# Two layers of feed-forward and attention on one core: attention's first tiles and maxima are issued within the feed-forward's last steps, and ScalarE sends the rows of the maxima

## The chip, the core and the metric

The kernel runs on one core of a Trainium2 chip. The core has TensorE (PE: matrix products, whose weight loads PEld overlap), VectorE (DVE), ScalarE (ACT), GpSimd (POOL) and SyncE (SP, which here only issues DMA transfers). Each engine works through its own instructions in order; they meet through semaphores. The metric is the device time of one execution in microseconds, median of the runs.

## What is computed

The input `x` has 2048 positions of 256 features, in f32. It goes through two "macaron" layers:

```
x = x + 0.5 * ffn0(layernorm(x));  x = x + attn0(layernorm(x));  x = x + 0.5 * ffn0(layernorm(x))   # layer 0: f0, attention, f1
x = x + 0.5 * ffn1(layernorm(x));  x = x + attn1(layernorm(x));  x = x + 0.5 * ffn1(layernorm(x))   # layer 1: f2, attention, f3
```

- `ffn0`: weights rounded to three values per group of 64, gate and up products to 1024 features, silu(gate) * up, RMS norm, down product.
- `ffn1`: the same gate and up form in f32, of each four hidden values the two with the largest magnitude are kept, then the down product.
- `attn0`, `attn1`: causal attention with 16 heads of 16 features. Layer 0 adds an ALiBi bias (slope of the head times key position minus query position); layer 1 has biases on q, k, v and output, and rotates q and k by position. Softmax, product with v, output projection.

## The kernel before

**Tiling.** Features lie on the partitions, positions along the free axis. Positions are cut into four chunks of 512 (`NCH`, `CH`), a chunk into four tiles of 128 (`T`). Attention works on 16 groups: group n is chunk n // 4 of the queries and four of the heads (n % 4). The phases follow each other: feed-forward f0, attention of layer 0, feed-forwards f1 and f2 in one run, attention of layer 1, f3.

**Feed-forward.** `feed_forwards` (L435) walks through the chunks, and through eight steps `f` per chunk. A step issues the gate and up products of 128 hidden features (L306 in layer 0: six pairs, as x is split in three bf16 parts; L281 in layer 1, f32), ScalarE's silu (L317) and VectorE's product (L318). In layer 0, VectorE also takes the parts of h (L334, L329), ScalarE squares (L339) and GpSimd sums (L340). The chunk's down products (L361 or L292) come in the next chunk's steps as a "tail". In layer 1, `sparsify` (L385) does the choice of two in four, with comparisons on VectorE (L394) and sums on GpSimd. Layer norms of the next phase run beside this from a list `background`. After each step a hook is called: `beside0` in f0, `beside1` in f1 and f2.

**Attention's preparation.** `attention` is a generator. Its first `next` opens the pool `ka` and yields another generator, `first()` (L618), which does chunk 0's work: `prep_qk(0, "k")`, `prep_qk(0, "q")`, `prep_v(0)`. `prep_qk` (L521) projects (L536, two halves), splits the f32 result in three bf16 parts (ScalarE L544 or L578, VectorE L545 or L579, ScalarE L580, GpSimd L581), and SyncE writes these to scratch in DRAM in six transfers (L585). Layer 1 comes with a bias (L547), a swap of the two 64-partition halves by DMA (L556) and the rotation (VectorE L571 and L577, GpSimd L575) ahead of the split. The hooks advance `first()` by one yield per step: in f0 in chunk 3's steps, in f2 from chunk 2's fifth step on. `attend` (L1032) runs what is left of it when the feed-forward has ended.

**Attention.** Then pools `kv` and `ap` are opened in the feed-forward's memory. `load` (L636) reads a group's q tile and a k tile (96 rows: head features in six product terms) back from DRAM, and constant rows below them (L640, L645). Query maxima come first: `mx_unit` (L663) takes scores with queries on the partitions (`pq`, L671, and a mask product L679), and VectorE reduces each 128x512 tile (L682). When a group has all its maxima, `mx_end` (L684) makes three bf16 parts of their negatives, and `mx_turn` (L699) transposes them on TensorE (L704), ScalarE copies (L712), and SyncE sends three rows into the q tile (L714), so that the second score product subtracts the maximum by itself. That second product has keys on the partitions (`st_pair`, L725: `pst`, L733), ScalarE takes the exponential (`pT`, L753), and four small products per head group add to the output (`pav`, L768), which VectorE and GpSimd divide by the sum (L789, L793, L794).

**What sets the order.** On the four compute engines the program's order is the order of the code (`manual_schedule`); only SyncE's transfers are ordered by the tile framework. `slots` (L829) lists one slot for each group and key block of 128. `maxima` (L835) puts units of maxima on slots. Slot -1 held group 0's four tiles and three tiles of group 1, seven units in all, ahead of the first slot (L912); after each of these units one step of chunk 1's preparation was taken. In the slots, `step` advances the preparation of the next chunk, and `need` drains it as far as a load asks for.

**Buffers that matter.** PSUM has two pairs of banks (`ps2`: gate/up products and `pst`), three single banks (`ps3`: `pq`, projections, means, down products, transposed maxima) and one bank for sums (`ps1`). The `kd` and `q` rings have four tiles each in `kv`.

Of the kernel before, what the change touches and what calls it, by code (L numbers as in the profile page):

```python
# [26 lines left out]
G = 4  # L27
# [19 lines left out]
def macaron_kernel(ctx: ExitStack, tc: tile.TileContext, a, out):  # L47
# [37 lines left out]
        )  # L85


    ident = cpool.tile([P, P], F32, name="ident")
    make_identity(nc, ident)
    ident_b = cpool.tile([P, P], BF16, name="ident_b")  # L90
    nc.vector.tensor_copy(ident_b, ident)

    mask_qk = cpool.tile([P, P], BF16, name="mask_qk")
    mask_kq = cpool.tile([P, P], BF16, name="mask_kq")
# [395 lines left out]
    def attention(layer, following):  # L490
# [9 lines left out]
        with ExitStack() as st:  # L500
# [20 lines left out]
            def prep_qk(c, what):  # L521

                ready(c)
                if what == "k" and c > 0:
                    nc.gpsimd.memset(va[c], 1.0)
                at = 0 if what == "q" else DC
                name = f"{layer}_{what}{c}"
                dn = ka.tile([P, DC, CH], F32, tag="dn", bufs=2 - layer, name=f"dn{name}")
                pt = [
                    ka.tile([P, DC, CH], BF16, tag=f"part{j}", bufs=1, name=f"p{j}{name}")  # L530
                    for j in range(3)
                ]
                for i in range(DC):
                    pp = ps_one(f"pp{name}_{i}")
                    for dc in range(DC):
                        nc.tensor.matmul(  # L536
                            pp,
                            lhsT=wqkv[:, dc, (at + i) * P : (at + i + 1) * P],
                            rhs=xns[c][:, dc, :],
                            start=dc == 0,  # L540
                            stop=dc == DC - 1,
                        )
                    if layer == 0:
                        nc.scalar.copy(pt[0][:, i, :], pp)  # L544
                        nc.vector.tensor_tensor(dn[:, i, :], pp, pt[0][:, i, :], ALU.subtract)  # L545
                    else:
                        nc.scalar.activation(  # L547
                            dn[:, i, :], pp, AF.Identity, bias=b_qk[:, at + i : at + i + 1]
                        )
                    if i == 0:  # L550
                        yield
                if layer == 1:

                    sw = ka.tile([P, DC, CH], F32, tag="sw", bufs=1, name=f"sw_{what}{c}")
                    for o in range(2):
                        nc.sync.dma_start(  # L556
                            out=sw[o * 64 : o * 64 + 64, :, :],
                            in_=dn[64 - o * 64 : 128 - o * 64, :, :],
                        )
                    if turns.get("of") != c:  # L560
                        turns["of"] = c
                        turns["cs"] = ka.tile(
                            [P, 2, CH], F32, tag="cs", bufs=1, name=f"cs_{what}{c}"
                        )
                        nc.sync.dma_start(
                            out=turns["cs"], in_=a["cos_sin"][:, :, c * CH : (c + 1) * CH]
                        )
                    cs = turns["cs"]
                    yield
                    yield  # L570
                    nc.vector.tensor_tensor(  # L571
                        dn, dn, cs[:, 0:1, :].to_broadcast([P, DC, CH]), ALU.mult
                    )
                    for i in range(DC):
                        nc.gpsimd.tensor_tensor(sw[:, i, :], sw[:, i, :], cs[:, 1, :], ALU.mult)  # L575
                    yield
                    nc.vector.tensor_tensor(dn, dn, sw, ALU.add)  # L577
                    nc.scalar.copy(pt[0], dn)  # L578
                    nc.vector.tensor_tensor(dn, dn, pt[0], ALU.subtract)  # L579
                nc.scalar.copy(pt[1], dn)  # L580
                nc.gpsimd.tensor_tensor(pt[2], dn, pt[1], ALU.subtract)  # L581
                for j in range(3):
                    for m, part in enumerate(Q_PARTS if what == "q" else K_PARTS):
                        if part == j:
                            nc.sync.dma_start(  # L585
                                out=parts[what, c][:, m, :, :].rearrange("i p t -> p i t"),
                                in_=pt[j],
                            )
                done.add((what, c))
                yield  # L590
# [24 lines left out]
                        done.add(("v", c))  # L615
                    yield

            def first():  # L618
                nc.gpsimd.memset(va[0], 1.0)
                yield  # L620
                for work in (prep_qk(0, "k"), prep_qk(0, "q"), prep_v(0)):
                    yield from work

            yield first()
            kv = st.enter_context(tc.tile_pool(name=f"kv{layer}", bufs=1))
            ap = st.enter_context(tc.tile_pool(name=f"at{layer}", bufs=2))
            va += [values(kv, c) for c in range(1, NCH)]
            acc = ps_acc(f"pav{layer}")
            zts = {}
            zs = {}  # L630


            qs = {}
            ks = {}

            def load(n, kc):  # L636
                c, g = divmod(n, G)

                def stack(to, what, of, extra):
                    nc.sync.dma_start(  # L640
                        out=to[0:RM],
                        in_=parts[what, of][g // 2]
                        .rearrange("m (d u) t -> (m d) u t", u=HB)[:, g % 2 * 4 : g % 2 * 4 + 4, :],
                    )
                    nc.sync.dma_start(out=to[RM:rows], in_=extra[0 : rows - RM])  # L645

                need("k", kc)
                ks[n, kc] = kv.tile(
                    [P, 4, CH], BF16, tag="kd" if kc == c else "ko", bufs=4 if kc == c else 5,
                    name=f"k{layer}_{n}_{kc}",  # L650
                )
                stack(ks[n, kc], "k", kc, a["k_rows"][c - kc])
                if n not in qs:
                    need("q", c)
                    qs[n] = kv.tile([P, 4, CH], BF16, tag="q", bufs=4, name=f"q{layer}_{n}")
                    stack(qs[n], "q", c, a["q_rows"][g])


# [4 lines left out]
            def mx_unit(n, t, kc, heads):  # L663

                c, g = divmod(n, G)
                if n not in mxs:
                    mxs[n] = ap.tile([P, T, 4, NCH], F32, tag="mx", bufs=4, name=f"mx{layer}_{n}")
                w = (t + 1) * P if kc == c else CH
                for hh in heads:
                    pq = ps_one(f"pq{layer}_{n}_{t}_{kc}_{hh}")[:, 0:w]  # L670
# [13 lines left out]
            def mx_end(n):  # L684


                c = n // G
                ng = ap.tile([P, T, 3, 4], F32, tag="neg", name=f"neg{layer}_{n}")
                nc.vector.tensor_reduce(
                    ng[:, :, 0, :], mxs.pop(n)[:, :, :, 0 : c + 1], AX.X, ALU.max, negate=True  # L690
                )
                top = ng.bitcast(BF16).rearrange("p t m (h two) -> p t m h two", two=2)[..., 1]
                for m in range(2):
                    nc.vector.tensor_tensor(
                        ng[:, :, m + 1, :], ng[:, :, m, :], top[:, :, m, :], ALU.subtract
                    )
                negs[n] = top

            def mx_turn(n):  # L699
# [3 lines left out]
                for t in range(T):  # L703
# [4 lines left out]
                        start=True,  # L708
                        stop=True,
                    )  # L710
                qx = ap.tile([12, CH], BF16, tag="qx", bufs=2, name=f"qx{layer}_{n}")
                nc.scalar.copy(qx, pt)  # L712
                for m in range(3):
                    nc.sync.dma_start(out=qs[n][RM + m : RM + m + 1, :, :], in_=qx[4 * m : 4 * m + 4, :])  # L714
                turned_max.add(n)


            def banks(name, apart):
# [161 lines left out]
            def need(*what):  # L880
                while what not in done:
                    assert preps, what
                    step()

            left = {}
            for units in maxima.values():
                for u in units:
# [17 lines left out]

            def load_to(slot):
                while uses and uses[0][1] <= slot:
                    load(*uses.popleft()[0])

            load_to(-1)  # L910
            preps.extend((prep_qk(1, "k"), prep_qk(1, "q"), prep_v(1)))
            for unit in maxima[-1]:  # L912
                mx_next(unit, (0, 1, 2, 3))
                step()
                now[0] += 1
                run_due()

            unsummed = deque()
            pairs = [0]
# [92 lines left out]

    def begin(layer, following):
        att = attention(layer, following)
        begun[:] = att, next(att)

    def beside0(s, at, f):
        if not quants and not begun:
            raw_scope.close()
            begin(0, "f1")  # L1020
        if at == NCH - 1:
            next(begun[1], None)

    def beside1(s, at, f):
        if s == 1 and at == 0 and f == FC // 2:
            own.close()
            ffn0_scope.close()
            begin(1, "f3")
        if s == 1 and (at == NCH - 1 or at == NCH - 2 and f >= FC // 2):
            next(begun[1], None)  # L1030

    def attend():  # L1032
        att, first = begun
        for _ in first:
            pass
        next(att, None)
        begun.clear()

# [126 lines left out]
```

## Time and profile before

| what | value |
|---|---|
| median of 3 runs | 1954.04 us (1952.93 to 1957.03) |
| profiled execution | 1957.69 us; its span 1955.7 us |
| TensorE | 1761.4 us busy, 90% of the span, mean granted clock 0.96 |
| VectorE | 1361.6 us, 70% |
| ScalarE | 894.2 us, 46% |
| GpSimd | 458.4 us, 23% |
| DMA | 93.10 MB, mean 48 GB/s |
| reductions of the maxima (L682) | 1280, 708.6 us, mean 603 ns |
| exponentials (L753) | 614, 542.6 us, mean 896 ns |
| rows of the maxima sent (L714) | 96 transfers of 4.0 KB, issued by SyncE |

The profile is of one execution. Busy time is that of instructions at work; an engine's idle time is put down to what released it ("releaser"), such as another engine's line or a DMA. "Granted clock" is the share of full speed that TensorE was allowed. In a timeline a row is a run of like instructions: start, length, engine, line, operation, out<-in, shape, and in brackets the idle time before it with its releaser. SPq and ACTq rows are the times in which SyncE or ScalarE issued a DMA.

### The profile page before, as it was taken

How to read it: one execution, taken by the hardware profiler on the slowest of the kernel's cores; microseconds unless marked ns; L12 is line 12 of the kernel's file. 1: busy time of each engine (PE TensorE's matmuls, PEld its weight loads, DVE VectorE, ACT ScalarE, POOL GpSimd, SP SyncE). 2: the span in 40 equal slices, each digit the busy share in tenths (PEclk: the TensorE clock that was granted, in tenths of full speed). 3: DMA queues.
4: the chain of work that ended last, by engine and by line, in shares of the span. 5: the costliest groups of instructions: out<-in, count | busy, mean ns of one | idle time of the engine just before them, and what ended most of it. 6: DMA issues, size and time to landing. Idle time of an engine off the chain costs nothing. (4 is left out here: it accounts for less than half of the span.)

```text
span 1955.7 us, 26994 instructions
## 1 busy us (share of the span) xinstructions
PE 1761.4 (90%) x10684; PEld 726.5 (37%) x10684; DVE 1361.6 (70%) x2384; ACT 894.2 (46%) x1112; POOL 458.4 (23%) x418
## 2 busy tenths in 40 slices
PE   5699789999999999789999876898999999998997
PEld 1233344433433333333444333433333333333443
DVE  7866377787788883666575655868877888825664
ACT  4343254555555668334422312445555656673220
POOL 3455321101000000455453432211111000003422
PEclk9799899999999999989999986999999999999999
DMA  4000252213211000200000115222122110000000
GB/s 129 1 1 33 82 148 83 73 54 102 62 45 46 28 28 2 73 1 0 1 11 0 54 61 158 82 73 92 52 69 86 43 43 26 18 1 0 11 11 22
DMA packets 50510, 93.10 MB, mean 48 GB/s; under 512 B 5424, under 2 KB 33072, under 8 KB 50128
## 3 DMA queue, kind: packets, MB, share of 16 engines
q1 hardware_dynamic: 49296, 89.28, 14.8%
q10 hardware_dynamic: 1088, 2.10, 0.3%
q8 instruction: 84, 1.38, 0.3%
q14 instruction: 42, 0.34, 0.1%
HBM read 59.51 MB, written 27.26 MB: 44 GB/s over the span
## 5 line engine op out<-in xcount | busy, mean ns | idle before, releaser
L682 DVE TENSOR_REDUCE mx<-pq 128x1 f32<-128x512 f32 (+3 forms) x1280 | 708.6, 603 | 158.5 <-PE pq L679 91.2
L753 ACT ACTIVATE pT<-pst 128x1024 f32<-128x1024 f32 (+3 forms) x614 | 542.6, 896 | 334.9 <-PE pst L733 196.8
L671 PE MATMUL pq<-k,q 105*128 105x512 bf16 (+7 forms) x1280 | 378.8, 353 | 74.7 <-DVE mx L682 52.3
L733 PE MATMUL pst<-q,k 99*128 99x512 bf16 (+7 forms) x1280 | 357.7, 354 | 5.1 <-ACT pT L753 4.2
L768 PE MATMUL pav<-pT,va 128*32 128x256 f32 (+1 forms) x4608 | 352.4, 382 | 5.2 <-DVE yt L789 5.0
L281 PE MATMUL pg_f<-xn,wgu 128*128 128x512 f32 x512 | 229.8, 602 | 11.5 <-DVE hr_f L318 11.5
L794 POOL TENSOR_TENSOR zt<-yt,rd 128x64 f32<-128x64 f32 x128 | 38.4, 300 | 795.2 <-DVE rd L793 795.1
L733 PEld LDWEIGHTS <-k 105*128 105x128 bf16 (+1 forms) x1280 | 101.5, 98 | 254.1 <-issue 218.4
L317 ACT ACTIVATE sl_f<-pg_f 128x512 f32<-128x512 f32 x128 | 76.0, 594 | 251.8 <-PE pg_f L281 175.0
L671 PEld LDWEIGHTS <-q 105*128 105x128 bf16 (+1 forms) x1280 | 124.5, 100 | 148.0 <-issue 44.3
L306 PE MATMUL pg_f<-xn,wgu 128*128 128x512 bf16 x512 | 156.2, 413 | 19.5 <-DVE wgu L170 6.8
L768 PEld LDWEIGHTS pav<-pT,va 128*32 128x32 f32 x4608 | 93.8, 108 | 208.7 <-issue 174.8
L281 PEld LDWEIGHTS pg_f<-xn,wgu 128*128 128x128 f32 x512 | 98.6, 193 | 136.9 <-issue 121.0
L306 PEld LDWEIGHTS <-wgu 128*128 128x128 bf16 x768 | 77.7, 101 | 166.9 <-issue 74.7
L292 PE MATMUL po_f<-h_f,wd 128*128 128x512 f32 x256 | 116.3, 608 | 17.3 <-DVE h_f L418 17.3
L340 POOL TENSOR_TENSOR ss_f<-ss_f,sq_f 128x512 f32<-128x512 f32 x56 | 91.1, 1628 | 111.5 <-ACT sq_f L339 111.3
L679 PE MATMUL pq<-mask_qk,ident_b 128*128 128x128 bf16 x512 | 107.3, 227 | 0.0
L741 PE MATMUL pst<-mask_kq,ident_b 128*128 128x128 bf16 x512 | 103.1, 222 | 0.0
L306 PE MATMUL pg_f<-xm_f,wgu 128*128 128x512 bf16 x256 | 85.3, 416 | 14.0 <-DVE xm_f L238 14.0
L318 DVE TENSOR_TENSOR h_f<-sl_f,pg_f 128x512 f32<-128x512 f32 x64 | 43.6, 682 | 76.4 <-ACT sl_f L317 76.3
L789 DVE STREAM_TRANSPOSE yt<-pav 128x128 f32<-128x128 f32 x128 | 39.8, 311 | 76.7 <-PE pav L768 76.7
L394 DVE TENSOR_TENSOR ge_f<-h_f 128x1536 bf16<-128x1536 f32 (+2 forms) x48 | 67.6, 1437 | 28.0 <-ACT h_f L387 28.0
(132 smaller groups left out, 1802.5 us busy)
## 6 DMA issues: line engine op xcount, KB each, us to landing
k<-dk SPq DMA_DIRECT2D x80, 384.0 KB
dk<-p_k SPq DMA_DIRECT2D x48, 256.0 KB
dq<-p_q SPq DMA_DIRECT2D x48, 256.0 KB
q<-dq SPq DMA_DIRECT2D x32, 384.0 KB
x<-in_xT ACTq DMA_DIRECT2D x4, 512.0 KB
raw<-in_w_gu SPq DMA_DIRECT2D x8, 256.0 KB
wgu<-in_w_gu SPq DMA_DIRECT2D x1, 2048.0 KB
cs_k<-in_cos_sin SPq DMA_DIRECT2D x4, 512.0 KB
```

The source lines that it names most:

```text
L281: nc.tensor.matmul(pg[:, half, :], lhsT=wgu[:, dc, half * F + f * P : half * F + (f + 1) * P], rhs=xn[:, dc, :], start=dc == 0, stop=dc == ...
L292: nc.tensor.matmul(po, lhsT=w[:, f, dc * P : (dc + 1) * P], rhs=h[:, f, :], start=f == 0, stop=f == FC - 1,)
L306: nc.tensor.matmul(pg[:, half, :], lhsT=wgu0[:, dc, half * F + f * P : half * F + (f + 1) * P], rhs=xp[part][:, dc, :], start=part == 0 an ...
L317: nc.scalar.activation(sl, pg[:, 0, :], AF.Silu)
L340: nc.gpsimd.tensor_tensor(ss, ss, sq, ALU.add)
L671: nc.tensor.matmul(pq, lhsT=qs[n][0:rows, hh, t * P : (t + 1) * P], rhs=ks[n, kc][0:rows, hh, 0:w], start=True, stop=kc < c,)
L679: nc.tensor.matmul(pq[:, w - P : w], lhsT=ident_b, rhs=mask_qk, start=False, stop=True)
L682: nc.vector.tensor_reduce(mxs[n][:, t, hh, kc : kc + 1], pq, AX.X, ALU.max)
L733: nc.tensor.matmul(ps[i][:, lo:CH], lhsT=ks[n, kc][0:rows, hh, t * P : (t + 1) * P], rhs=qs[n][0:rows, hh, lo:CH], start=True, stop=kc < c,)
L741: nc.tensor.matmul(ps[i][:, lo : lo + P], lhsT=ident_b, rhs=mask_kq, start=False, stop=True)
L753: nc.scalar.activation(pT[:, :, lo:CH], pair[:, :, lo:CH], AF.Exp, scale=0.25)
L768: nc.tensor.matmul(acc[hh * SLOT : (hh + 1) * SLOT, a:b], lhsT=va[kc][:, t, v0 : v0 + SLOT], rhs=pTs[hh // 2][:, hh % 2, a:b], start=kb == ...
```

## The change

1. `first()` now has more in it: after chunk 0's k and q it issues the loads of groups 0 and 1 (`load(0, 0)`, `load(1, 0)`), after v the seven units of maxima that were in slot -1, in halves of two heads with a yield after each, `mx_end` and `mx_turn` of group 0, and then chunk 1's k and q preparation.
2. A new `go_on` takes two yields per step, from the fifth step of chunk 2 on, for both layers. `attend` runs `first()` only until the maxima are done; what is left of it goes to the head of `preps`.
3. So that the loads can come before `kv` exists, groups with n % 4 of 0 and 1 have their k and q tiles in `ka`, two of each; 2 and 3 have two of each in `kv`. The maxima, negatives and `qx` are in `ka` too, with 3, 1 and 1 buffers instead of 4, 2 and 2.
4. The three transfers of a group's maxima rows are issued by ScalarE instead of SyncE, for all groups.
5. The ones in `va` of chunks 1 to 3 are set at attention's start instead of in `prep_qk`, and the bf16 identity is made directly.

```diff
-    ident = cpool.tile([P, P], F32, name="ident")
-    make_identity(nc, ident)
     ident_b = cpool.tile([P, P], BF16, name="ident_b")
-    nc.vector.tensor_copy(ident_b, ident)
+    make_identity(nc, ident_b)
...
+            pools = [ka]
+            def ring(n, other=False):
+                return pools[0 if other or n % 4 > 1 else -1]
...
-                need("k", kc)
-                ks[n, kc] = kv.tile(
-                    [P, 4, CH], BF16, tag="kd" if kc == c else "ko", bufs=4 if kc == c else 5,
+                ks[n, kc] = ring(n, kc < c).tile(
+                    [P, 4, CH], BF16, tag="kd" if kc == c else "ko", bufs=2 if kc == c else 5,
...
-                    need("q", c)
-                    qs[n] = kv.tile([P, 4, CH], BF16, tag="q", bufs=4, name=f"q{layer}_{n}")
+                    qs[n] = ring(n).tile([P, 4, CH], BF16, tag="q", bufs=2, name=f"q{layer}_{n}")
...
-                    nc.sync.dma_start(out=qs[n][RM + m : RM + m + 1, :, :], in_=qx[4 * m : 4 * m + 4, :])
+                    nc.scalar.dma_start(out=qs[n][RM + m : RM + m + 1, :, :], in_=qx[4 * m : 4 * m + 4, :])
...
+            def first():
+                nc.gpsimd.memset(va[0], 1.0)
+                yield
+                for work in (prep_qk(0, "k"), prep_qk(0, "q")):
+                    yield from work
+                load(0, 0)
+                yield from prep_v(0)
+                load(1, 0)
+                for n, t in FIRST:
+                    for heads in ((0, 1), (2, 3)):
+                        mx_unit(n, t, 0, heads)
+                        yield
+                    if (n, t) == (0, T - 1):
+                        mx_end(0)
+                        yield
+                        mx_turn(0)
+                        yield
+                done.add("maxima")
+                for work in (prep_qk(1, "k"), prep_qk(1, "q")):
+                    yield from work
+            FIRST = [(0, t) for t in range(T)] + [(1, t) for t in (2, 1, 0)]
...
-            load_to(-1)
-            preps.extend((prep_qk(1, "k"), prep_qk(1, "q"), prep_v(1)))
-            for unit in maxima[-1]:
-                mx_next(unit, (0, 1, 2, 3))
-                step()
-                now[0] += 1
-                run_due()
+                    (n, kc), _ = uses.popleft()
+                    if (n, kc) not in ks:
+                        need("k", kc)
+                        need("q", n // G)
+                        load(n, kc)
+            preps.extend((beginning, prep_v(1)))
...
+    def go_on(s, at, f):
+        if at == NCH - 1 or at == NCH - 2 and f >= FC // 2:
+            for _ in range(2):
+                next(begun[1], None)
...
     def attend():
-        att, first = begun
-        for _ in first:
-            pass
+        att, first, done = begun
+        while "maxima" not in done:
+            next(first)
```

More of the change, by code (lines that the diff above doesn't have):

```diff
@@ L523, in prep_qk @@
                 ready(c)
-                if what == "k" and c > 0:
-                    nc.gpsimd.memset(va[c], 1.0)
                 at = 0 if what == "q" else DC
@@ L616, in prep_v @@
                     yield
[L618 to L630, printed above, removed]
+            pools = [ka]
             qs = {}
             ks = {}
+            def ring(n, other=False):
+                return pools[0 if other or n % 4 > 1 else -1]
             def load(n, kc):
@@ L666, in mx_unit @@
                 if n not in mxs:
-                    mxs[n] = ap.tile([P, T, 4, NCH], F32, tag="mx", bufs=4, name=f"mx{layer}_{n}")
+                    mxs[n] = ka.tile([P, T, 4, NCH], F32, tag="mx", bufs=3, name=f"mx{layer}_{n}")
                 w = (t + 1) * P if kc == c else CH
@@ L687, in mx_end @@
                 c = n // G
-                ng = ap.tile([P, T, 3, 4], F32, tag="neg", name=f"neg{layer}_{n}")
+                ng = ka.tile([P, T, 3, 4], F32, tag="neg", bufs=1, name=f"neg{layer}_{n}")
                 nc.vector.tensor_reduce(
@@ L710, in mx_turn @@
                     )
-                qx = ap.tile([12, CH], BF16, tag="qx", bufs=2, name=f"qx{layer}_{n}")
+                qx = ka.tile([12, CH], BF16, tag="qx", bufs=1, name=f"qx{layer}_{n}")
                 nc.scalar.copy(qx, pt)
                 for m in range(3):
-                    nc.sync.dma_start(out=qs[n][RM + m : RM + m + 1, :, :], in_=qx[4 * m : 4 * m + 4, :])
+                    nc.scalar.dma_start(out=qs[n][RM + m : RM + m + 1, :, :], in_=qx[4 * m : 4 * m + 4, :])
                 turned_max.add(n)
+            def first():
[19 more added lines that the diff above has]
+            FIRST = [(0, t) for t in range(T)] + [(1, t) for t in (2, 1, 0)]
+            beginning = first()
+            yield beginning, done
+            kv = st.enter_context(tc.tile_pool(name=f"kv{layer}", bufs=1))
+            ap = st.enter_context(tc.tile_pool(name=f"at{layer}", bufs=2))
+            pools.insert(0, kv)
+            va += [values(kv, c) for c in range(1, NCH)]
+            for c in range(1, NCH):
+                nc.gpsimd.memset(va[c], 1.0)
+            acc = ps_acc(f"pav{layer}")
+            zts = {}
+            zs = {}
             def banks(name, apart):
@@ L883, in need @@
                     step()
+            assert sorted(maxima.pop(-1)) == sorted((n, t, 0) for n, t in FIRST)
             left = {}
@@ L907, in load_to @@
                 while uses and uses[0][1] <= slot:
-                    load(*uses.popleft()[0])
-            load_to(-1)
-            preps.extend((prep_qk(1, "k"), prep_qk(1, "q"), prep_v(1)))
-            for unit in maxima[-1]:
-                mx_next(unit, (0, 1, 2, 3))
-                step()
-                now[0] += 1
-                run_due()
+                    (n, kc), _ = uses.popleft()
[4 more added lines that the diff above has]
+            preps.extend((beginning, prep_v(1)))
             unsummed = deque()
@@ L1014, in begin @@
         att = attention(layer, following)
-        begun[:] = att, next(att)
+        begun[:] = att, *next(att)
+    def go_on(s, at, f):
+        if at == NCH - 1 or at == NCH - 2 and f >= FC // 2:
+            for _ in range(2):
+                next(begun[1], None)
     def beside0(s, at, f):
@@ L1020, in beside0 @@
             begin(0, "f1")
-        if at == NCH - 1:
-            next(begun[1], None)
+        go_on(s, at, f)
     def beside1(s, at, f):
@@ L1028, in beside1 @@
             begin(1, "f3")
-        if s == 1 and (at == NCH - 1 or at == NCH - 2 and f >= FC // 2):
-            next(begun[1], None)
+        if s == 1:
+            go_on(s, at, f)
     def attend():
-        att, first = begun
-        for _ in first:
-            pass
+        att, first, done = begun
+        while "maxima" not in done:
+            next(first)
         next(att, None)
```

## The prediction

> **What bounds the kernel now.** I read the busy time by stretch first, then TensorE's waits in the two stretches that hand a feed-forward over to attention, then the timelines. Columns of the first fence: stretch, length, busy time of PE, PEld, DVE, ACT, POOL, granted TensorE clock, DMA share, GB/s.
>
> ```profile
> 150.00:267.00 117.00, 96.33 (x381) 43.92 (x380) 62.13 (x93) 35.03 (x55) 45.75 (x30) 0.91 0.26 81
> 267.00:812.00 545.00, 519.20 (x4266) 207.21 (x4265) 411.33 (x834) 317.12 (x388) 49.14 (x85) 0.99 0.19 60
> ...
> 1050.00:1224.00 174.00, 137.38 (x378) 63.57 (x377) 98.61 (x139) 41.86 (x48) 63.03 (x42) 0.86 0.26 77
> 1224.00:1778.00 554.00, 519.15 (x4190) 207.48 (x4189) 408.45 (x822) 312.80 (x375) 55.85 (x90) 0.98 0.17 52
> ```
>
> TensorE sets the time almost everywhere (95% and 94% busy in the two attentions). Only at the two hand-overs does it not: 20.7 us idle of 117 in layer 0 and 36.6 of 174 in layer 1, with the clock at 0.91 and 0.86. So the change is judged there. Waits in these stretches (total, times, longest), layer 0, then layer 1:
>
> ```profile
> PE pq L671 <- DMA q<-in_q_rows: 8.7, 1, 8.7
> PE pss_f L353 <- POOL ss_f L340: 4.0, 1, 4.0
> PE pg_f L306 <- DVE xm_f L238: 2.2, 1, 2.2
> ```
>
> ```profile
> PE pq L671 <- DVE mx L682: 12.6, 5, 8.1
> PE po_f L292 <- DVE h_f L418: 10.3, 1, 10.3
> PE pg_f L281 <- DVE hr_f L318: 5.9, 1, 5.9
> PE pq L671 <- DMA q<-in_q_rows: 4.4, 1, 4.4
> ```
>
> The change aims at the first line of layer 0: the first score tile waits 8.7 us for q and k, whose pool opens only when the feed-forward has ended. The price of a long gap stands right behind it:
>
> ```profile
> 240.25 0.27 PE L671 MATMUL pq<-k,q 105*128 105x128 bf16 x1 [8.71 <-DMA q<-in_q_rows]
> ...
> 241.27 3.78 PE L536 MATMUL pp_k<-xn,wqkv 128*128 128x512 f32 x4
> ...
> 247.11 1.98 PE L536 MATMUL pp_k<-xn,wqkv 128*128 128x512 f32 x4
> ```
>
> The same four rows (two f32 products) take 3.78 us after the gap and 1.98 when warm: 1.9 us more, and about 2 us in all before full speed returns. What a q tile needs between its projection and its first use, in SyncE's queue and in the chain of waits:
>
> ```profile
> 201.71 4.99 SPq L585 DMA_DIRECT2D dq<-p_q  x6
> ```
>
> ```profile
> 1230.05 5.23 DMA q<-dq
> ```
>
> The q projection ended at 200.9, the six writes of its parts to DRAM were issued up to 206.7, and a read back takes 5.2 us from issue to use (also 5.5 at 234.71). Nothing of this was on TensorE's path before: the feed-forward ran on for 24 us. That is the cover that the change takes away.
>
> **The moved steps, layer 0.** The instruction orders show it: TensorE works in order, and chunk 0's q now ends one and a half steps before the first score tile, which stands ahead of the next gate/up product. I count from the start of chunk 2's fifth gate/up product (151.1 before). A gate/up step is 2.7 us, a projection half or v half 1.72, a mean 0.9. Then q's second half ends at 15.9; v 1.7, gate/up 2.7 and v 1.7 follow, so TensorE reaches score tile (0,0) at 22.0. The q chain meanwhile: ScalarE has chunk 1's Square first and converts at 18.4 to 19.0; VectorE has chunk 3's split (1.2+1.3) first and subtracts till 20.6; ScalarE's cast (1.04) till 21.7; GpSimd's subtraction (2.14) till 24.3; last write issued 24.8, landed 27.3 (estimate: 2.5, as DMA traffic of the dq writes before died out about 2 us after the last issue), read 5.2: 32.5. **TensorE stalls 10.5 us in the midst of the feed-forward**, and 2.0 cold.
>
> Next, each moved step brings up to four score tiles, but ps3 has three banks. The fourth tile waits until VectorE has reduced the first, and VectorE's reductions are queued behind the step's silu, product, difference and last part (0.6+3x0.7) and often a transpose. Going through the order I get waits of 1.7, 3.1, 0.8, 2.7 and 3.2 us at chunk 3's steps 0, 1, 2, 5, 6: 11.5. Steps 3 and 4, with two tiles, wait nothing. The wait for the sum of squares (4.0) shrinks to 2.4, as two tiles and a projection lie in it.
>
> What goes: the load's 8.7 and its cold clock 2; the split's 2.9 and 1.6 cold, now under the new stall; about 5 of small waits between the seven first units. Work only moves. In sum the first tile pair of key block 2 (275.6 before, 124.5 on my count) comes at 122.1, with all of chunk 1's projections done: **2 us won**.
>
> **The moved steps, layer 1.** Here q also passes through a half-swap by DMA, GpSimd and the rotation. A swap needs 4.4 us from issue to GpSimd (1184.06 to 1188.48), GpSimd's two multiplications 2.5 to 3.5, then VectorE, ScalarE, VectorE, ScalarE at 1.1 to 1.2 each, GpSimd 2.1, and the DRAM trip. Counting from chunk 2's fifth step (1054.75), steps 3.43, down projections 6.86: q's projection ends at 34.3 and TensorE is at the first score tile at 50. The chain: ScalarE is held by k's two casts until 37.3, then has a silu and an Abs (1.9), so q's bias comes at 42.1; swap landed 47.2; GpSimd has four sparsifying operations first, till 52.6, swap product till 55.3; four hops till 60; GpSimd till 62.2, writes issued 62.6, landed 65.1, read 5.2: 70.3. **Stall 20 us, 2 cold.** Then fourth tiles: 4.8, 2.3, 3.5 and 1.3 (the reductions stand behind comparisons of 1.8 and chains that wait for the down projection). The wait before the last down projections falls from 10.3 to 4.6, since no cast blocks the last silu; 5.9 (hr), 4.4 (load), and the 2.0+3.4 between units go.
>
> Then comes a bunch. Group 4's first load needs chunk 1's q, so the rest of chunk 1's k and q is drained in one place, after slot 0: all projections adjacent on TensorE, and in VectorE's and ScalarE's queues k's chain, then q's, ahead of group 2's reductions and the next exponentials. Two swap chains in series, q's behind k's writes in SyncE's queue: swap 4.5, GpSimd 3.2, four hops 4.6, GpSimd 2.1, bias 1.3; swap 4.5, GpSimd 3, three hops 3.6: about 27, of which TensorE has 3.5 of work: **23.5 us idle, 2 cold**. Before, the same chains were spread over the units and cost 8.2+2.0+3.4 and cold time. TensorE's losses (idle and slow) to key block 2's first pair: before 51 of 169.4 us (118 of work); after 22+12+1.5+6.6+25.5, that is 67.6. **17 us lost.** The Trainium skill ("TensorE: Matmul & The Clock Gate", Part 1) says that the clock halves after an idle window of about 3.4 us. By it the 1.3 to 3.2 us waits are free of cold time; the row here disagrees (after 2.2 and 0.7 us at 165 a pair took 1.05 for 0.61). I take the row only for the 4.8 one: 1.5; by the row everywhere it would be 6 more.
>
> **ScalarE sends the rows.** Three issues per group move from SyncE; columns start, length:
>
> ```profile
> 606.39 0.57 ACT L712 CAST qx<-ptm 12x512 bf16<-12x512 f32 x1 [0.35 <-PE ptm L704]
> ...
> 606.87 0.58 ACT L753 ACTIVATE pT<-pst 128x512 f32<-128x512 f32 x1
> ...
> 606.99 1.82 SPq L714 DMA_DIRECT2D q<-qx  x3
> ...
> 608.24 0.60 ACT L753 ACTIVATE pT<-pst 128x512 f32<-128x512 f32 x1 [0.79 <-PE pst L741]
> ```
>
> The skill's page "DMA: Bandwidth & Descriptors" ("Issuing engines are not separate DMA queues") says that using another engine saves issue time, usually small. By that the edit is worth about 0. The row says 1.82 us of a queue per group, and on ScalarE exponentials stand behind it. No row shows a wait of this kind on ScalarE, but its x loads bound it:
>
> ```profile
> 18.40 0.90 ACTq L83 DMA_DIRECT2D x<-in_xT  x2
> 18.88 0.61 ACT L152 ACTIVATE sg<-raw 128x512 bf16<-128x512 f32 x1
> 19.33 0.48 ACTq L83 DMA_DIRECT2D x<-in_xT  x1
> 19.84 1.28 ACT L317 ACT_TABLE_LOAD   x1 [0.35 <-issue]
> ```
>
> The table load starts only when the issue ends, so issues do hold ScalarE up. At 606 the exponential of 606.87 would start at 607.9 and the next end at 609.1; TensorE's next pair but one (608.88 before) needs that bank: 0.5 us late, then the slack of 0.5 to 0.8 us per half slot catches up. Bounds per group: 0 to 1.8 us; 0.5 is nearest to the rows. In chunks 0 and 1 TensorE waits for VectorE anyway, so 16 groups count: **8 us lost**. SyncE's loads no longer queue behind these rows: a gain of at most 1.9 (one wait for q<-dq), I take 1. The identity without copy, rings of two and two instead of four, fewer buffers (mx 3, neg 1, qx 1, whose users are a group apart) and earlier memsets (3x1.05 on GpSimd, under waits for DMA): nothing; if a cover failed, 2 us.
>
> **Sum:** -2+17+8-1 = +22. The working is in one execution's time, 1957.69 (span 1955.7); the median of three is 1954.04, and I put the difference on that: 1976.
>
> **Rivals.**
> - *The moved work fits (faster).* If the q tile lands before TensorE gets there, both mid-stage stalls vanish: -12.5 and -22, sum -12.5: 1941.5. For it: 8.7 and 4.4 us of load wait really go. Against: it needs a chain of at most 6 us (layer 0) and 16 (layer 1) from the projection's end, and I count 17 and 36. It decides from there.
> - *Layer 1's bunch overlaps.* If chains cost half of what I count in queue waits, layer 1 loses about 0: 1957 or so, no change.
> - *ScalarE pays in full:* 1.8 in all 30 groups outside the feed-forward is 54 instead of 8; at half, for slack, 27: -2+17+27-1 = +41, so 1995.
> - That the tiles don't move is excluded by the instruction order.
>
> **Numbers.** The forecast 1976 has 0.62 (1964 to 1990 by itself: read 4 to 6 us, chain hops, cold time); fit 0.14, overlap 0.12, full ScalarE price 0.12. Faster by over 0.2% (3.9 us, about what a measurement can tell) 0.14, within 0.06, slower 0.80 (the overlap case splits in two). Range 1955 to 1996.
>
> **What would show it.** Right: TensorE's longest waits are the first pq (q<-dq, about 10 us near 173 and 20 near 1105), pg and po waits shrink, pq<-mx totals rise in the feed-forward's steps, one wait of about 23 us follows slot 0 of layer 1, and short pst<-pT waits appear at each qx. Wrong: the first pq waits under 3 us, or pT never starts late after the DMAs on ScalarE.

## The result and the profile after

The changed kernel takes 2009.44 us (median of 4 runs, 2005.68 to 2014.98) against 1953.75 (4 runs beside it, 1952.93 to 1957.03): ratio 1.0277, 95% interval 1.0262 to 1.0292. It is slower, as forecast, but by 54 to 56 us and not by 22, and so above the range (1955 to 1996). The profiled execution has a span of 2006.4 us.

The four stretches of the changed kernel that answer to those shown of before, with the same columns; their ends are moved as far as the instructions there have moved:

```profile
150.00:275.00 125.00, 94.68 (x387) 42.56 (x386) 57.01 (x100) 35.35 (x52) 44.34 (x31) 0.91 0.22 67
275.00:827.00 552.00, 518.76 (x4249) 208.64 (x4249) 408.16 (x826) 313.85 (x389) 49.62 (x84) 0.99 0.20 61
1067.00:1263.00 196.00, 133.59 (x378) 61.35 (x377) 98.97 (x139) 41.50 (x48) 65.38 (x44) 0.86 0.25 75
1263.00:1828.00 565.00, 523.26 (x4189) 208.87 (x4187) 408.85 (x822) 311.59 (x375) 53.84 (x88) 0.97 0.16 48
```

The hand-over of layer 0 leaves 30.3 us idle of 125 (20.7 of 117 before), that of layer 1 62.4 of 196 (36.6 of 174). But the two attentions have grown as well, though the moved steps lie outside them: 545 to 552 us and 554 to 565. TensorE's waits in the hand-over of layer 0 (here up to the first tile pair of key block 2, at 284.01), then in layer 1's:

```profile
PE pq L656 <- issue: 8.7, 1, 8.7
PE pq L656 <- DVE dn_q L541: 6.1, 1, 6.1
PE pq L656 <- DVE tt_rms_f L204: 4.4, 1, 4.4
PE pq L656 <- DVE mx L667: 4.1, 1, 4.1
PE pq L656 <- DVE xc_after_f L253: 2.7, 1, 2.7
PE pss_f L351 <- POOL ss_f L338: 1.9, 1, 1.9
```

```profile
PE pq L656 <- DVE mx L667: 22.5, 4, 10.8
PE pq L656 <- DMA q<-dq: 18.6, 1, 18.6
PE pq L656 <- ACT dn_q L543: 12.4, 1, 12.4
PE po_f L290 <- DVE h_f L416: 5.3, 1, 5.3
```

The 8.7 (put down to "issue") and the 18.6 us are the stalls of the first score tile in the midst of the feed-forward (forecast 10.5 and 20). The 12.4, and the longest of the `mx` waits, 10.8, are the bunch after slot 0 of layer 1: 12.4+10.8 = 23.2 us (forecast 23.5, as one wait). The 6.1 us in layer 0 has no term in the forecast. ScalarE around it:

```profile
265.60 1.04 ACT L576 CAST p_k<-dn_k 128x1024 bf16<-128x1024 f32 x1 [0.76 <-DVE dn_k L541]
274.03 1.07 ACT L540 CAST p_q<-pp_q 128x512 bf16<-128x512 f32 x2 [7.39 <-DMA dk<-p_k]
276.01 1.04 ACT L576 CAST p_q<-dn_q 128x1024 bf16<-128x1024 f32 x1 [0.91 <-DVE dn_q L541]
```

In layer 0 the bunch stands there too. Chunk 1's k and q share one buffer for each of their three parts. The cast of q's first part (274.03) waits 7.4 us until k's writes to DRAM have read that buffer, and behind the cast stands VectorE's subtraction that frees a score bank for TensorE.

To part cold time from waiting, TensorE's rows in layer 1:

```profile
1142.07 0.29 PE L656 MATMUL pq<-k,q 99*128 99x128 bf16 x1 [18.60 <-DMA q<-dq]
...
1142.47 6.04 PE L279 MATMUL pg_f<-xn,wgu 128*128 128x512 f32 x8
...
1155.32 0.37 PE L656 MATMUL pq<-k,q 99*128 99x256 bf16 x1 [6.41 <-DVE mx L667]
...
1155.59 6.29 PE L279 MATMUL pg_f<-xn,wgu 128*128 128x512 f32 x8
...
1186.53 0.38 PE L656 MATMUL pq<-k,q 99*128 99x512 bf16 x1 [2.97 <-DVE mx L667]
...
1186.80 3.65 PE L279 MATMUL pg_f<-xn,wgu 128*128 128x512 f32 x8
```

The same eight rows of a gate/up product take 6.04 us behind the gap of 18.6, 6.29 behind 6.4, and 3.65 behind 3.0 (also 3.65 behind one of 2.3, at 1171.61). The gap of 3.0 is not always free. With one edit elsewhere (e1_sync_rows, below) the same wait at the same place leaves 5.35:

```profile
1174.21 0.38 PE L656 MATMUL pq<-k,q 99*128 99x512 bf16 x1 [2.97 <-DVE mx L667]
...
1174.48 5.35 PE L279 MATMUL pg_f<-xn,wgu 128*128 128x512 f32 x8
```

### The profile page after: what moved, and what is told of

The parts are those of the page before. It is cut to its first block, busy times and chain, and to the rows that moved or that the text cites. A ratio compares the mean times of both kernels' runs of the same rounds, so it can differ in the third digit from the quotient of the medians.

```text
span 2006.4 us, 26941 instructions
## 1 busy us (share of the span) xinstructions
PE 1761.7 (88%) x10684; PEld 726.5 (36%) x10684; DVE 1355.5 (68%) x2383; ACT 891.6 (44%) x1112; POOL 458.5 (23%) x418
## 5 line engine op out<-in xcount | busy, mean ns | idle before, releaser
L753 PE MATMUL pst<-q,k 99*128 99x512 bf16 (+7 forms) x1280 | 359.0, 354 | 18.9 <-ACT pT L773 18.8
L304 PE MATMUL pg_f<-xn,wgu 128*128 128x512 bf16 x512 | 161.7, 424 | 18.9 <-DVE wgu L168 6.8
L316 DVE TENSOR_TENSOR hr_f<-sl_f,pg_f 128x512 f32<-128x512 f32 x64 | 43.6, 682 | 65.7 <-ACT sl_f L315 65.7
```

What stands on the lines that cost most here:

```text
L304: nc.tensor.matmul(pg[:, half, :], lhsT=wgu0[:, dc, half * F + f * P : half * F + (f + 1) * P], rhs=xp[part][:, dc, :], start=part == 0 an ...
L316: nc.vector.tensor_tensor(to, sl, pg[:, 1, :], ALU.mult)
L753: nc.tensor.matmul(ps[i][:, lo:CH], lhsT=ks[n, kc][0:rows, hh, t * P : (t + 1) * P], rhs=qs[n][0:rows, hh, lo:CH], start=True, stop=kc < c,)
```

## The experiments

Each run is compared by its ratio to the kernel before, timed beside it; 0.001 of ratio is 1.95 us. Differences between two ratios are uncertain by some 4 us. To see where in the program time is lost I also use the casts of the rows of maxima (ScalarE, `qx`): there is one per group, and its start in a trace shows how late that group is. Each such figure is from one profiled execution, and that of the kernel before (1957.69) lies 3.6 us above its median.

**What ScalarE's sending costs.** One edit on either kernel:

```
-                    nc.scalar.dma_start(out=qs[n][RM + m : ...
+                    nc.sync.dma_start(out=qs[n][RM + m : ...
```

> The changed kernel with its rows of the maxima sent by SyncE again; all moved steps stay. The forecast's theory (0.5 us in each of 16 groups, less 1 of relief on SyncE): 7 us faster than the changed kernel, about 2002 us. The rival, read from the changed kernel's trace (0.6 us more per group in every group of chunks 2 and 3 of both layers, two jumps of 2.5 and 3.6 in layer 1, and some in chunk 1): 14 to 18 us faster, 1992 to 1995 us. If the skill's rule holds (only issue time, small): 2009 us.

Measured: 1980.59 us, ratio 1.0149 (1.0127 to 1.0171), 25 us less than the changed kernel. The reverse edit on the kernel before:

> The kernel before with one edit: ScalarE sends the rows of the maxima. Nothing is moved. Forecast's theory: 7 us slower than before, 1961 us. The trace's rival: 14 to 18 us slower, 1968 to 1972 us, with short waits of pst for pT at each group in chunks 1 to 3. The rule of small issue time: 1954 us. If the price only shows together with the moved steps (rings of two, later start), this run is under 5 us slower while the reverse edit on the changed kernel wins more than that.

Measured: 1975.91 us, 1.0129 (1.0111 to 1.0146): 25 us more. So the price is the same with and without the moved steps, three times the forecast's 8, and above even my reading of the trace. That row-sending is a cost of its own is shown. Where it arises is seen in TensorE's waits of chunks 0 and 1 of layer 0, before and with the one edit:

```profile
PE pq L671 <- DVE mx L682: 9.2, 23, 1.5
PE pst L733 <- ACT pT L753: 1.3, 2, 0.9
```

```profile
PE pq L671 <- DVE mx L682: 8.6, 22, 1.5
PE pst L733 <- ACT pT L753: 6.6, 5, 2.5
```

The score pairs wait 6.6 us for `pT` instead of 1.3, while the waits for VectorE hardly change (9.2 to 8.6): the new waits don't hide behind those. Over the whole execution TensorE's waits for `pT` rise by 16.3 us (4.2 to 20.5), and the span by 18.5. One group on ScalarE, before and with the edit:

```profile
351.94 0.57 ACT L712 CAST qx<-ptm 12x512 bf16<-12x512 f32 x1 [1.18 <-PE ptm L704]
353.87 0.65 ACT L609 COPY va<-pv 128x256 f32<-128x256 f32 x2 [1.35 <-PE pv L598]
```

```profile
353.76 0.57 ACT L712 CAST qx<-ptm 12x512 bf16<-12x512 f32 x1 [1.18 <-PE ptm L704]
354.37 2.15 ACTq L714 DMA_DIRECT2D q<-qx  x3
356.55 0.65 ACT L609 COPY va<-pv 128x256 f32<-128x256 f32 x2 [2.22 <-DMA q<-qx]
```

Before, the copy of v starts 1.9 us after the cast; now the three issues hold the queue 2.15 us and it starts 2.8 us after. Then a dose, on the kernel before:

```
+                    eng = nc.scalar if m == 0 else nc.sync
+                    eng.dma_start(out=qs[n][RM + m : ...
```

> The kernel before, with ScalarE sending one of the three rows of each group's maxima and SyncE the other two. It doses the cost of ScalarE's sending: all three rows cost 24 us. If what counts is the time that ScalarE's queue is held beyond a slack of about 1.2 us per group, one issue (0.6 us) hides: within 3 us of before. If each issue is paid alike: about 8 us slower, 1960 us. If the fixed part counts (the first issue waiting until the cast of the row is written): 15 to 20 us slower, 1967 to 1972 us.

Measured: 1954.61 us, 1.0000 (0.9989 to 1.0012). One issue per group is free. With `m < 2`:

> The kernel before, with ScalarE sending two of the three rows and SyncE one. One row cost nothing (ratio 1.000), three cost 24 us. By a slack of about 1.1 us of ScalarE's queue in each of 31 groups: two issues (1.22 us) cost 3 to 6 us, 1957 to 1960 us. If the price is in the third issue's place alone, or two rows are paid in proportion: 12 to 16 us, 1966 to 1970 us.

Measured: 1968.01 us, 1.0074 (1.0055 to 1.0093), 14 us. My slack of 1.1 us would have made it 3 to 6. The number falls in the range that I gave to a price in proportion, but one issue that costs nothing excludes that: 0, 14 and 25 us for one, two and three issues mean a slack of about one issue in the mean of the groups. The groups are not alike, though. TensorE's waits for `pT` with none, one, two and three issues, whole execution:

```profile
PE pst L733 <- ACT pT L753: 4.2, 7, 0.9
PE pst L734 <- ACT pT L754: 6.0, 8, 1.3
PE pst L734 <- ACT pT L754: 11.0, 15, 2.2
PE pst L733 <- ACT pT L753: 20.5, 26, 2.5
```

Of these, 0.5, 0.9, 1.6 and 6.4 us fall in chunks 2 and 3 of both layers. There two issues nearly hide, and the third is the one that costs. In chunks 0 and 1 and outside the attentions (3.7, 5.1, 9.4 and 14.1 us) the second costs already. Last, the groups (`eng = nc.scalar if n // G > 1 else nc.sync`):

> The kernel before, with ScalarE sending the rows only in the groups of chunks 2 and 3 of both layers. The forecast said that these 16 groups carry the whole cost (24 us measured for all): then 22 to 24 us slower than before, 1977 us. The rival, read from the times of the casts in the run with the one edit, that every group pays about 0.6 us, those of chunks 0 and 1 and the hand-over too: 8 to 12 us slower, 1964 us.

Measured: 1967.02 us, 1.0073 (1.0054 to 1.0092), 14 us of the 25. By this ratio the groups of chunks 2 and 3 pay 0.9 us each (0.7 to 1.1), not 0.5; by the waits and the casts of the traces it is 0.4 to 0.6. What is left, about 11 us by difference, falls to chunks 0 and 1, which I had put at nothing.

**The bunch of layer 0.**

```
-                    ka.tile([P, DC, CH], BF16, tag=f"part{j}", bufs=1, ...
+                    ka.tile([P, DC, CH], BF16, tag=f"part{j}" + (what if layer == 0 else ""), ...
```

> The changed kernel, but in layer 0 the three part tiles of q and of k have a buffer each instead of one in common. The theory from the trace: in the bunch after slot 0 of layer 0 ScalarE waits 7.4 us until k's six writes to DRAM have read the parts, and TensorE stands 6.1 us behind that; both go, 6 to 8 us faster than the changed kernel, 2002 us. The rival: the wait is only covered up, and TensorE then waits for VectorE's or GpSimd's part of the same chain in that place: within 2 us of 2009.

Measured: 2001.01 us, 1.0250 (1.0233 to 1.0268), 5 us less by ratio, 7 by the spans. ScalarE's wait of 7.4 us for k's writes is gone from its list. By the casts, group 1 comes 10.2 us earlier than in the changed kernel and the last group of layer 0 5.5 us: part is given back in the later groups.

**The score tiles in the feed-forward.** The feed-forward stops calling `first()` once the loads are issued, so the tiles follow in one row when it has ended:

```
+                load(1, 0)
+                done.add("loads")
                 ...
             for _ in range(2):
-                next(begun[1], None)
+                if "loads" not in begun[2]:
+                    next(begun[1], None)
```

> The changed kernel, but the feed-forward's last steps go only as far as the loads of groups 0 and 1; the score tiles and the maxima come in one row when the feed-forward has ended, and chunk 1's q and k in the slots as before. The forecast's theory: the stalls for q (10.5+2 and 20+2 us) and the waits of fourth tiles (11.5 and 12) go; small waits between the tiles (5 and 5.4), the sum of squares (1.6), the split (4.5), the last down products and gate (5.7 and 5.9) come back; the bunch after slot 0 stays. Net about 27 us faster than the changed kernel, 1982 us. The rival, that these tiles cost the same wherever they stand because VectorE's reductions set their pace and the bunch is what the change costs: under 10 us faster, 2000 us or more.

Measured: 1990.22 us, 1.0200 (1.0184 to 1.0215), 15 us less than the changed kernel and not 27. Its trace shows why: with no `yield` behind the loads, the first half tile still stood in each feed-forward, and both stalls with it:

```profile
PE pq L656 <- DMA q<-dq: 21.9, 4, 18.8
...
PE pq L656 <- issue: 8.5, 1, 8.5
```

With a `yield` behind the mark no tile is left there:

> As e4_units_back, where half a score tile of each layer had stayed in the feed-forward and TensorE waited 8.5 and 18.8 us for its q: now no score tile at all stands there, only the projections and the loads. The forecast's theory: both stalls and their cold clock (2 each) are a pure loss and go, as the loads land under the feed-forward: 31 us faster than e4_units_back, about 1959 us. The rival: the stall only gives time to VectorE and ScalarE, which are then late at the feed-forward's next waits (down product, gate, sum of squares), and half of it comes back: 1975 us or more.

Measured: 1966.77 us, 1.0077 (1.0053 to 1.0102), 24 us less than the run before it. The two waits are gone from TensorE's list, and most of their time (8.5+18.8 and 2 each for the cold clock, 31) is won, but not all: the waits of gate/up products for `hr` rise from 7.3 to 15.7 us. Half a tile per layer in the wrong place cost more than the places of all the other tiles (15).

**What is left of the change when its costs are undone.** As that run, with SyncE's rows and parts apart:

> As e6_no_early_tile, with SyncE sending the rows and with q's and k's parts in buffers of their own in layer 0. If the prices add (26 and 8 us, measured one by one): 34 us faster than e6_no_early_tile, about 1925 us by the forecast's theory of the stall, and so faster than before by 27 us; what is kept of the change is then the early loads (13 us of load waits) and the early pools. If they don't add, the bunch after slot 0 (23 us idle in layer 1) holds it at 1945 to 1955 us.

Measured: 1944.94 us, 0.9953 (0.9938 to 0.9968): faster than before by 9 us. The step from 1966.77 is 24 us by ratio and not 34 (30, if the two prices are taken by ratio too). By the casts the last group comes 23 us earlier, of which 2 are won by group 1 of layer 0 and the rest grows from group to group, as the price of the sending does; the parts gave little here, since in e6_no_early_tile TensorE's wait behind q's cast in layer 0 was 1.8 us and not 6.1. Chunk 1's q and k now taken in turn with the tiles:

```
         while "maxima" not in done:
             next(first, None)
+            count += 1
+            if count % 2 == 0:
+                next(second, None)
```

> As e7_loads_only, with chunk 1's q and k no longer drained in one place after slot 0 but taken one step after every two half tiles, as in the kernel before. The forecast's theory (the bunch's two swap chains in series idle TensorE 23.5 us and 2 cold in layer 1, against 8.2+2.0+3.4 when spread): 12 us faster than e7_loads_only, of which the part in layer 0 is about 2. The rival: chunk 1's chain also stands in front of the tiles' reductions on VectorE, so nothing is won: within 3 us.

Measured: 1942.72 us, 0.9946 (0.9929 to 0.9963): no difference to be told. By the casts it loses 6 us in layer 0 and wins 3.7 in layer 1. So only in layer 1:

> As e7_loads_only, with chunk 1's q and k taken in turn with the tiles (as e8_interleaved) in layer 1 only, since by the traces interleaving won about 4 us in layer 1 and lost 6 in layer 0. If the layers are independent: 1940 to 1941 us, 0.7% faster than before. If what layer 0 loses was given back later: 1943 to 1945 us, as the two runs before it.

Measured: 1937.33 us, 0.9919 (0.9902 to 0.9936), 16 us faster than before, the fastest version of the study. TensorE's waits in layer 1's hand-over, first with the bunch (e7_loads_only), then without:

```profile
PE pq L659 <- ACT dn_q L546: 12.4, 1, 12.4
PE pq L659 <- DVE mx L670: 11.0, 2, 10.8
...
PE ptm L692 <- DVE neg L682: 2.0, 1, 2.0
```

```profile
PE pq L659 <- DVE mx L670: 12.5, 4, 10.0
...
PE ptm L692 <- DVE neg L682: 5.5, 1, 5.5
...
PE pq L659 <- ACT dn_q L546: 0.5, 1, 0.5
```

The chain's 12.4 us goes, but TensorE waits longer for the tiles' own reductions and for the negated maxima (11.0+2.0 becomes 12.5+5.5). Of the bunch, then, 4 us (by the casts) to 7 (by the ratios) can be had, and not the 12 that I had counted.

Last, are tiles in the feed-forward worth something when their q is there? They start on the fifth step after the loads (`HOLD = 4`), which leaves room for two whole tiles in each layer:

```
+            if "loads" in begun[2]:
+                waited[0] += 1
+                if waited[0] <= HOLD:
+                    return
```

> As e7_loads_only, but score tiles stand in the feed-forward again, from the fifth step behind the one that issues the loads: by then q has landed (TensorE stood 8.5 and 18.9 us for it when they stood right behind). Room is left for two whole tiles in each layer, in the last two steps. It asks whether moved tiles gain anything when their q is there. If the stall was all that made them dear: 2 of 7 tiles, some 3 us of TensorE's time and waits per layer, lie under the feed-forward: 1939 us against 1945. The forecast's term of the fourth tile (three score banks, reductions queued on VectorE behind the steps' work; 1.7 to 4.8 us each time): nothing won or up to 6 us lost, 1945 to 1951 us.

Measured: 1946.94 us, 0.9959 (0.9943 to 0.9975) beside 0.9953 without them. Nothing is won, at least with two of the seven tiles. In layer 0's hand-over TensorE waits for the tiles' reductions instead of the sum of squares:

```profile
PE pq L659 <- DVE mx L670: 8.4, 4, 2.7
PE pq L659 <- DVE xc_after_f L253: 2.6, 1, 2.6
```

```profile
PE pss_f L351 <- POOL ss_f L338: 6.2, 1, 6.2
...
PE pq L659 <- DVE mx L670: 0.7, 2, 0.5
```

The first fence is with two tiles in the feed-forward, the second without.

## Why the prediction missed

The direction was right, and so were the waits in the hand-overs that I could count by hand. Of the four terms of the sum -2+17+8-1, the first and the third were far too small: they measured about +7, +22, +25 and nothing that could be told, 54 in all.

- **ScalarE sends the rows, +8: the step that failed most.** "In chunks 0 and 1 TensorE waits for VectorE anyway, so 16 groups count" was wrong. Measured: 25 us in all, 14 in those 16 groups (chunks 2 and 3) and 11 in the others. The waits for VectorE in chunks 0 and 1 stayed (9.2 and 8.6 us in layer 0) and the waits for `pT` came beside them, so they give no cover. "0.5 is nearest to the rows" was too small by the ratio (0.9), but about right by the traces (0.4 to 0.6). Its working has a slip: three issues of 1.82 us from 606.99 on hold the next exponential until 608.8, not 607.9. With the edit it came 2.0 us later (613.18, where 611.2 would be unchanged), and TensorE's wait there was close to the 0.5:

```profile
613.18 1.46 ACT L753 ACTIVATE pT<-pst 128x512 f32<-128x512 f32 x3 [1.92 <-DMA q<-qx]
613.83 0.22 PE L733 MATMUL pst<-q,k 105*128 105x128 bf16 x1 [0.58 <-ACT pT L753]
```

  My bound "at half, for slack, 27" was the right size, and I gave it 0.12; its even price in 30 groups is not what the traces show, so the match is in part luck. By the Trainium skill's page "DMA: Bandwidth & Descriptors", section "Issuing engines are not separate DMA queues", another engine saves only issue time, usually small against the transfer; that weighs the gain and says nothing of the price on the engine that takes over. Here 1.84 us of issues per group cost 25 us over 32 groups, and one issue of 0.6 us cost none.
- **Layer 0, -2: measured about +7** (offset of layer 0's last cast in e1_sync_rows, without ScalarE's rows). The stall was 8.75 (forecast 10.5), the waits of tiles in the feed-forward 13.1 (11.5), the sum of squares 1.9 (2.4). What failed is "with all of chunk 1's projections done": done on TensorE, but their chain in ScalarE's queue was not. I looked at the bunch only in layer 1 and passed over the shared part buffers, 6.1 us of idle TensorE and 5 to 7 us of the time. The rest is a slip in the sum: by its terms 10.5+2+11.5 come in and 8.7+2+2.9+1.6+5+1.6 go, which is 2.2 lost, not 2 won. The count to 122.1 beside it holds 4 us for which no term is given; the tile pair came at 132.7 (284.01 less 151.29, where the fifth product starts).
- **Layer 1, +17: measured +22** (28.6 at the last cast less the 6.7 of layer 0). Idle time came nearly as counted: 62.4 us against the 20+12+4.6+23.5 = 60.1 in the sum. What is more is mostly slow time: from the fifth product on (1071.9) the stretch is 191.1 long, so 128.7 were busy with what I had put at 118 of work, 10.7 more, where the sum held 67.6-60.1 = 7.5. The gap of 6.4 us cost 2.6 (6.29-3.65) where I had taken 1.5, and the bunch, priced at 2 as one gap, came as two of 12.4 and 10.8 with slow rows behind each. On the rule weighed there, the page "TensorE: Matmul & The Clock Gate" of the Trainium skill, Part 1 (the clock halves after an idle window of about 3.4 us), would make the waits of 2.3 and 3.0 free; by the row that I held against it, both would have cost something. The traces side with neither. Every gap over 3.3 us in the hand-overs of the two kernels left slow rows behind it. The one of 2.3 left none, and the one of 3.0 cost nothing in the changed kernel and 1.7 us (5.35-3.65) in e1_sync_rows. What sets these shorter gaps apart stays open.
- **SyncE's relief, -1**: not told apart. It is part of the net 25 us that the edit costs on either kernel.
- **Smaller rings and fewer buffers, nothing**: this held in the attentions. With SyncE's rows (e1_sync_rows) the casts of layer 0 stand 8.0 us behind the kernel before at group 4 and 6.7 at group 15, those of layer 1 28.2 at group 5 and 28.6 at group 15. So the growth of the two attentions is the price of the rows.
- **The rival "the moved work fits"** named the right condition, q landing before TensorE is there. Even so met, for two tiles, it wins nothing (e9_tiles_after_landing). What the change does win shows only where these costs are undone and no tile stands early: 9 us, and 16 with layer 1's chain spread.

The sum held no term for a bunch in layer 0, and the costliest edit was priced from one group at one place; both left the range too narrow.

What stays open: why the second issue already costs in chunks 0 and 1, and why the times put the groups of chunks 2 and 3 dearer than the traces do (their difference is about the uncertainty of 4 us); and how much of the last runs' gain is the early loads and how much the pools opened early or the moved memsets and the shorter making of the identity, which no run parted.

## What to carry over

Before work is moved ahead of a wait into a busy stretch, find when its operand lands there: half a tile per layer placed too early cost 24 us, while the change without early tiles and with its other costs undone won 9. A DMA issue on an engine that feeds TensorE is not free: price it by that engine's slack per unit of work, in every unit, since the slack differs between them; here one issue of three hid everywhere, and two nearly hid in chunks 2 and 3. Where two chains are drained in one place, look for the single buffer that they share.

## What the runs showed of the hardware

- Three issues held ScalarE's queue 1.84 to 2.15 us, and the next operation there started only behind the last of them (356.55, wait 2.22), though it used other data. In chunks 2 and 3 that cost 0.4 to 0.9 us per group (traces and times).
- A longer gap on TensorE did not cost more: behind 6.4 us the next product was 2.6 us slower, behind 18.6 it was 2.4. Behind 2.3 us it was not slower, and behind 3.0 us once not and once by 1.7.
